# Moving stage d of the last three batches in the order of a fused transformer and RWKV block

## The chip, the core and the metric

The kernel runs on one core of a Trainium2 chip. The metric is the time of one execution on the device in microseconds, given as the median of several runs. One execution was also profiled; the lines quoted in this document come from its trace, in which time runs from the first instruction (0) to the last one (the span).

The engines are called as in the profile: PE (TensorE, matmuls), PEld (its weight loads), DVE (VectorE), ACT (ScalarE), POOL (GpSimd) and SPq (the queue of SyncE, from which this kernel issues its DMAs).

## The reference

Eight sequences (batches) of 256 tokens with 512 channels pass through two layers. The first is a transformer block with self-attention, cross-attention and an MLP. The second, in which the change lies, has a time mixing with a recurrence over the tokens in 32 heads of 16 channels, and a channel mixing:

```python
xk, xw, xv, xr, xg = ...                      # mixes of the normed input and its shift
w = jnp.exp(-jnp.exp(time_decay + jnp.tanh(xw @ td_w1) @ td_w2))
r, k, v, g = xr @ Wr.T, xk @ Wk.T, xv @ Wv.T, silu(xg @ Wg.T)
def step(s, rkvw):
    a = k_t[..., :, None] * v_t[..., None, :]
    out = jnp.einsum('bhi,bhij->bhj', r_t, u * a + s)
    s = a + w_t[..., :, None] * s
    return (s, out)
og = groupnorm(out) * gn_w + gn_b
x1 = x + og * g @ Wo.T
xc = _ln(x1, ln2_w, ln2_b)
xk2, xr2 = xc + sx2 * ffn_maa_k, xc + sx2 * ffn_maa_r
rr = jax.nn.sigmoid(xr2 @ Wfr.T)
kk = jnp.square(jax.nn.relu(xk2 @ Wfk.T))
return x1 + rr * (kk @ Wfv.T)
```

## The kernel before, in words

All large products are made of three matmuls each (`mm3`, L189 to L193): both factors are split into a high and a low part. The attention and MLP stages of all batches come first; the two mixings of the second layer follow and overlap with the end of the MLP.

**Time mixing** (class `TimeMix`) has five stages for a batch b. `a` norms the input and makes the small mixing factors. `b` and `e` project gate, key, value, decay and receptance and store them in DRAM. The recurrence is cut into chunks of 16 tokens: `c` (from L695) computes inside all chunks at once on POOL (products `X`, L720 to L762) and DVE (their sums, L722 to L769). It loads the values into two staging buffers (`vh`, L708 and L709) and ACT copies them into `vt` (L710), which takes a buffer of the tag `in`. `c` stores its results in DRAM (`back`, L771 to L777). `d` (from L780) is "the stage between chunks": it carries the state from chunk to chunk. It loads the chunk decays `dd` (`dn`, L784) and transposes them on PE (L787, tile `wtp`), forms the chunks' updates with 256 small matmuls (L814, tile `up`), transposes the receptance (`to_t`, L223 and L823, tile `wtp` again), scans over the chunks on DVE (L831), multiplies with 256 small matmuls (L841), adds to `c`'s output (L844), norms by heads (L850 to L868) and stores `yg` (L854).

**Channel mixing** (class `ChannelMix`) has six units for a batch: `p` (gate and transposes of `yg`), `o` (output projection, residual, norm), `t` (transposes and the two mixes, L937 to L943; the mix for `fr` is written to a tile `o`, the one for `fk` in place), `r` (product with `fr`, L950), `k` (product with `fk`, L959 to L962) and `v` (product with `fv`, L970 and L971). `p0` also loads the four weight matrices.

**What sets the order.** The program is written down stage by stage in the order of the string `SEQ` (L71). A compile-time scheduler then fixes each engine's order by priorities: a stage's priority is that of its batch plus its entry in `AT` (L86), so that `d` of batch b goes ahead of all channel mixing, and `p` to `v` follow by batch. Two things are added. `in_turn` (L874) puts the PE instructions of `o`, `t`, `r`, `k` and `v` behind the last matmul of the unit written before it, with `tc.issue_after`, which fixes the order of issue on PE and adds no wait for the end. And buffers are shared by tags: `SLOTS` (L54) and `BANKS` (L77) give each tile of a stage a tag, most with one buffer; `wst` is a pool of two buffers with one tag. The tags that matter here:

- PSUM bank k5: `wtp` of stage `d` (four tiles for a batch) and `o` of the unit `t` (two tiles).
- pool `wst` (`staged`, L543): two tiles `vh` of each `c`; five tiles of each `d`: `dn`, two tiles with the values (L799 to L801, loaded in L692), two with the receptance (L821).
- tag `in` (a16 to a19): three inputs and `vt` of each `c`, with one buffer each.

In the order before, `d5` stands between `c6` and `c7`, `d6` after `o0`, `d7` after `r0`, and no PE instruction of a `d` stands behind a unit.

Of the kernel before, what the change touches and what calls it, by code (L numbers as in the profile page):

```python
# [1 line left out]

# [15 lines left out]
P = 128  # L18
# [21 lines left out]
def slots(text):  # L40
# [28 lines left out]


SEQ = (  # L71
# [3 lines left out]
)  # L75

# [15 lines left out]
def r32(ap):  # L92
    return ap.bitcast(F32)
# [3 lines left out]
def block_kernel(ctx: ExitStack, tc: tile.TileContext, a: dict, out: bass.AP):  # L97
    nc = tc.nc
    NB = out.shape[0]
    V, S, G, TE = nc.vector, nc.scalar, nc.gpsimd, nc.tensor  # L100
# [12 lines left out]
    ident = r32(identr)  # L113
# [19 lines left out]
    def wt(name, shape, dt=F32):  # L133
        tag = name
        if name in SLOTS[phase[0]]:
            tags = SLOTS[phase[0]][name]
            i = turn.get((phase[0], name), 0)
            turn[phase[0], name] = i + 1
            tag = tags[i % len(tags)]
        return wk.tile(shape, dt, name=name, tag=tag)  # L140

    def bank(kind, shape):
        kind = {"attn": {"tp": "mm", "o": "mm", "out": "mm"}, "time": {"mp": "tp"}}.get(phase[0], {}).get(kind, kind)
        tags = BANKS[phase[0]][kind]
        i = turn.get((phase[0], kind, "bank"), 0)
        turn[phase[0], kind, "bank"] = i + 1
        return psp.tile(shape, F32, name=kind, tag=tags[i % len(tags)])
# [39 lines left out]
    latest = [None]  # L187
# [26 lines left out]
            V.tensor_scalar(xn[:, t, :], x[:, t, :], mv[:, t, 0:1], rstd[:, t : t + 1], ALU.subtract, ALU.mult)  # L214
        return xn

    def to_t(xn, emit, kind="tp"):

        for k2 in range(2):
            tp = bank(kind, [P, 2, T])  # L220
            for kk in range(2):
                for t in range(2):
                    latest[0] = TE.transpose(tp[:, kk, t * P : (t + 1) * P], xn[t][:, (2 * k2 + kk) * P : (2 * k2 + kk + 1) * P], ident)  # L223
            emit(k2, tp)

    def both(x):
# [196 lines left out]
    class SelfAttention:  # L423
# [23 lines left out]
        def d(self, b, cx):  # L447
            if b == 0:
                W[0, "row"] = load_row("bao")
            x = load_x(a["x"][b], "xr")  # L450
            add_row(x, W[0, "row"])
            residual_out([W[0, "o"]], [cx], x, x1[b])
# [75 lines left out]
            residual_out(self.w2, hs, x, x2p[b] if self.half == 0 else x3[b])  # L528


    def shifted(xc, st, b, sx):

        G.tensor_tensor(sx[:, :, 1:], xc[:, :, : T - 1], xc[:, :, 1:], ALU.subtract)
        G.tensor_tensor(sx[:, :, 0:1], st[:, :, b : b + 1], xc[:, :, 0:1], ALU.subtract)
        return sx
# [7 lines left out]
    def staged(shape):  # L543
        return wst.tile(shape, F32, name="w")

    class TimeMix:
# [233 lines left out]
        def d(self, b, got):  # L780

            ksd, r0d, dd, vd, ond = got
            dn = staged([16, D])
            nc.sync.dma_start(out=dn.rearrange("c (e d) -> c e d", e=8), in_=dd.rearrange("e c d -> c e d"))  # L784
            dt_ps = bank("wtp", [P, KC, 16])
            for k in range(KC):
                TE.transpose(dt_ps[:, k, :], dn[:, k * P : (k + 1) * P], ident[:16, :16])  # L787
            dts = wt("dts", [P, KC, 16])

            G.memset(dts[:, :, 0:1], 0.0)  # L790
            S.copy(dts[:, :, 1:16], dt_ps[:, :, 0:15])
            s0t = wt("s0t", [P, KC, 16])
            nc.sync.dma_start(out=s0t, in_=a["ctx"][b, 2:18, :].rearrange("r (a j) -> (r a) j", j=16).rearrange("(g p) j -> p g j", p=P))
            centred(s0t.rearrange("p g j -> p (g j)"), KC, bank("wtp", [P, KC]))
            ks = [self.n_tile(ksd, t, "ks") for t in range(2)]

            vms = []
            for t in range(2):
                vms.append(wt("vm", [P, 2, D]))  # L799
                vn = self.n_tile(vd, t)  # L800
                for par in range(2):  # L801
                    S.activation(vms[t][:, par, :], vn, AF.Copy, scale=pm[:, 2 + par : 3 + par])

            sts = wt("sts", [P, KC, 32, 16])
            for hp in range(2):
                S.activation(sts[:, :, 16 * hp : 16 * hp + 16, 0], s0t, AF.Copy, scale=pm[:, hp : hp + 1])
            for r_ in range(4):
                rws = slice(32 * r_, 32 * r_ + 32)
                up = bank("up", [P, 2, KC, 2, 32])
                for t in range(2):  # L810
                    for g in range(KC):
                        for q in range(4):
                            ch = slice(g * P + 32 * q, g * P + 32 * q + 32)
                            TE.matmul(up[32 * q : 32 * q + 32, t, g], ks[t][rws, ch], vms[t][rws, :, ch], start=True, stop=True)  # L814
                for t in range(2):
                    c0 = 1 + 8 * t + 2 * r_
                    n = min(2, 16 - c0)
                    for hp in range(2):
                        js = slice(16 * hp, 16 * hp + 16)
                        S.activation(sts[:, :, js, c0 : c0 + n].rearrange("p g j c -> p g c j"), up[:, t, :, 0:n, js], AF.Copy, scale=pm[:, hp : hp + 1])  # L820
            r0 = [self.n_tile(r0d, t) for t in range(2)]  # L821
            r0t = wt("r0t", [P, KC, T])
            to_t(r0, lambda k2, tp: S.copy(r0t[:, 2 * k2 : 2 * k2 + 2, :], tp), "wtp")  # L823
            o = wt("on_", [P, 2, D])
            for t in range(2):
                nc.sync.dma_start(out=o[:, t, :].rearrange("p (e d) -> p e d", e=8), in_=ond[:, t * P : (t + 1) * P, :].rearrange("e p d -> p e d"))
            for g in range(KC):
                dT = bank("up", [P, 32, 16])
                S.copy(dT, dts[:, g, :].unsqueeze(1).broadcast_to([P, 32, 16]))
                sv = sts[:, g].rearrange("p j c -> p (j c)")  # L830
                V.tensor_tensor_scan(sv, dT.rearrange("p j c -> p (j c)"), sv, 0.0, ALU.mult, ALU.add)  # L831

            for q in range(4):
                rws = slice(32 * q, 32 * q + 32)
                op = bank("up", [P, 2, KC, 32, 2])
                for t in range(2):
                    for g in range(KC):
                        for pr in range(4):
                            c0 = 8 * t + 2 * pr
                            at = t * P + 32 * pr  # L840
                            TE.matmul(op[32 * pr : 32 * pr + 32, t, g], r0t[rws, g, at : at + 32], sts[rws, g, :, c0 : c0 + 2], start=True, stop=True)  # L841
                ov = o.rearrange("p t (g q j) -> p (t g) q j", q=4, j=32)[:, :, q]
                for par in range(2):
                    V.scalar_tensor_tensor(ov, op.rearrange("p t g j c -> p (t g) j c")[:, :, :, par], pm[:, 2 + par : 3 + par], ov, ALU.mult, ALU.add)  # L844

            oh = heads(o)
            gn = bank("up", [P, 3, 64])
            for t in range(2):
                sq = wt("sq", [P, D])
                S.activation(sq, o[:, t, :], AF.Square)  # L850
                V.tensor_reduce(gn[:, 0, 32 * t : 32 * t + 32], sq.rearrange("p (h j) -> p h j", j=16), AX.X, ALU.add)
            r = rsqrt(gn)
            V.tensor_tensor(oh, oh, r.unsqueeze(2).broadcast_to([P, 64, 16]), ALU.mult)
            nc.sync.dma_start(out=tok(yg[b]), in_=o)  # L854
# [14 lines left out]
        return v  # L869


    last = [None]

    def in_turn(unit):  # L874

        with ExitStack() as turns:
            if last[0] is not None:
                turns.enter_context(tc.issue_after(last[0].ins))
            unit()
        last[0] = latest[0]  # L880

# [14 lines left out]
    class ChannelMix:  # L896
# [7 lines left out]

        def p(self, b):
            if b == 0:
                for n in ("o", "fr", "fk", "fv"):
                    W[n] = load_unit(a["w" + n])
                W["st0"] = wt("st0", [P, KC, NB])
                nc.sync.dma_start(out=W["st0"], in_=a["st0"])  # L910
            yn = wt("yn", [P, 2, D])
            nc.sync.dma_start(out=yn, in_=tok(yg[b]))
            g = wt("g", [P, KC, T])
            nc.sync.dma_start(out=g, in_=gt[b])
            self.yt[b] = yt = parts()

            def gated(k2, tp):
                ks = scaled(tp, k2, "gn")
                V.scalar_tensor_tensor(tp, tp, 0.5, g[:, ks, :], ALU.mult, ALU.mult)
                split_ps(yt, ks, tp)  # L920

            to_t(both(yn), gated)
# [138 lines left out]
```

## Time and profile before

| | |
|---|---|
| three runs | 1967.8, 1974.79, 1980.11 us |
| median | 1974.79 us |
| the profiled execution's own time | 1970.55 us |
| its span | 1968.8 us |
| mean granted clock of TensorE | 0.927 |
| busy: PE, DVE, ACT, POOL | 88%, 70%, 56%, 38% |

In the profile a line `L787 PE MATMUL wtp<-ident,w` names the line of the kernel, the engine, the operation, and the tile written and the tiles read (numbers at the end of names are left out, so `o` and `o2` read the same). `<-` behind an idle time names what ended it.

When the stages run: the starts of L787, one for each `d`, are at 1317, 1384, 1452, 1519, 1582, 1650, 1714 and 1755 us; the last reduction L769 of a `c` starts at 1578 (c4), 1648 (c5), 1711 (c6) and 1774.5 us (c7); `v` ends at 1781 for batch 0 and then about every 26 us, at 1965 for batch 7.

### The profile page before, as it was taken

Reading aid. Unit: us, or ns where it says so; the run is one execution under the profiler, and the core shown is the slowest. Engines: PE = TensorE matmul, PEld = TensorE weight load, DVE = VectorE, ACT = ScalarE, POOL = GpSimd, SP = SyncE. Lnnn points to the kernel's source line nnn. Section 1 sums busy time; section 2 is a strip of 40 time slices with the busy share of each in tenths; the row PEclk is TensorE's granted clock in tenths of the full one; section 3 lists DMA queues with packets and bytes.
Section 4 is the critical chain, followed back from the end, with each engine's and each line's share of the span. In section 5 each row is a group of like instructions: output and inputs, shape, how many; then the busy total and the mean of one; then the engine's idle time right before and its main releaser. Section 6 shows DMA issues by size and latency. Waiting matters only on the chain.

```text
span 1968.8 us, 38833 instructions
## 1 busy us (share of the span) xinstructions
PE 1722.7 (88%) x14576; PEld 1450.2 (74%) x14576; DVE 1376.8 (70%) x3211; ACT 1104.7 (56%) x2745; POOL 745.0 (38%) x550
## 2 busy tenths in 40 slices
PE   4999999999899998999999998888798885279997
PEld 4777777777787776799999986676677664267876
DVE  4777777776778687655654344669779887688664
ACT  3877777887778787632332334344454455254553
POOL 2111111121222221222321100798999999990000
PEclk9999999999999998999999998989898877578999
DMA  6744444656555557322311123364556577434331
GB/s 189 166 121 119 119 118 124 186 147 164 131 144 137 150 129 208 111 79 79 115 65 65 54 102 108 106 163 136 156 138 164 145 199 230 138 93 129 114 101 54
DMA packets 241521, 255.74 MB, mean 130 GB/s; under 512 B 156547, under 2 KB 159499, under 8 KB 241334
## 3 DMA queue, kind: packets, MB, share of 16 engines
q1 hardware_dynamic: 241334, 253.26, 46.4%
q8 instruction: 115, 1.88, 0.4%
q14 instruction: 72, 0.59, 0.1%
HBM read 122.91 MB, written 63.18 MB: 95 GB/s over the span
## 4 chain that ended last, share of the span: by engine, by line
PE 56%; DVE 15%; POOL 12%; DMA 5%; ACT 5%; issue 4%; SPq 3%; DVEq 0%; POOLq 0%; ACTq 0%
POOL X L762 7%; PE o L192 7%; PE o L191 7%; PE o L193 7%; PE mm L191 5%; PE mm L192 4%; PE mm L193 4%; PE tr L372 3%; PE out L193 3%; PE out L192 3%; PE out L191 3%; DVE e L365 3%; PE cx L381 2%; DVE e L363 2%; PE sc L361 2%
## 5 line engine op out<-in xcount | busy, mean ns | idle before, releaser
L368 ACT ACTIVATE e<-e,mx 128x256 f32<-128x256 f32 x512 | 256.8, 506 | 43.3 <-DVE mx L365 42.3
L363 DVE TENSOR_TENSOR e<-sc,mc 128x512 f32<-128x512 f32 x256 | 172.5, 685 | 106.8 <-PE sc L361 55.9
L233 POOL TENSOR_TENSOR u<-y,u 128x1024 fp32r<-128x1024 f32 x32 | 78.4, 2449 | 440.4 <-ACT u L232 410.3
L365 DVE CUSTOM_DVE_ANT_0 e<-e,mn 128x256 f32<-128x256 f32 x512 | 223.3, 480 | 1.0
L762 POOL TENSOR_TENSOR X<-A,in 128x128 f32<-128x128 f32 (+14 forms) x120 | 209.3, 1784 | 5.5 <-DVE ob L769 3.5
L372 PE MATMUL tr<-ident,e 128*128 128x128 f32 x1024 | 174.0, 285 | 17.3 <-ACT e L368 14.2
L191 PE MATMUL mm<-u,whi 128*128 128x256 f32 x512 | 154.3, 302 | 13.1 <-DVE s L325 6.6
L376 ACT COPY pt<-tr 128x512 f32<-128x512 f32 x256 | 146.7, 581 | 31.8 <-PE tr L372 31.0
L372 PEld LDWEIGHTS tr<-ident,e 128*128 128x128 f32 x1024 | 122.1, 144 | 48.0 <-ACT e L368 23.1
L191 PE MATMUL o<-whi,s 128*128 128x512 f32 x320 | 137.6, 430 | 15.8 <-ACT s L639 8.4
L192 PE MATMUL mm<-u,whi 128*128 128x256 f32 x512 | 147.4, 288 | 4.0 <-POOL u L233 4.0
L191 PE MATMUL o<-u,whi 128*128 128x256 f32 x512 | 144.5, 286 | 3.5 <-ACT whi L175 2.1
L193 PE MATMUL mm<-u,wlo 128*128 128x256 f32 x512 | 147.5, 288 | 0.0
L192 PE MATMUL o<-u,whi 128*128 128x256 f32 x512 | 144.0, 282 | 0.0
L193 PE MATMUL o<-u,wlo 128*128 128x256 f32 x512 | 143.9, 283 | 0.0
L299 POOL TENSOR_TENSOR xr<-xr,row 128x512 f32<-128x512 f32 x48 | 64.8, 1371 | 187.5 <-DMA xr<-in_x 81.0
L361 PE MATMUL sc<-stk 128*128 128x256 f32 x512 | 117.3, 321 | 21.1 <-DVE e L363 16.0
L192 PE MATMUL o<-wlo,s 128*128 128x512 f32 x320 | 133.4, 417 | 0.0
L193 PE MATMUL o<-whi,s 128*128 128x512 f32 x320 | 129.8, 416 | 0.8 <-DVE s L894 0.8
L514 ACT ACTIVATE hf<-o,cv 128x256 f32<-128x256 f32 x128 | 59.7, 474 | 118.0 <-PE o L193 115.2
L203 POOL TENSOR_SCALAR rstd<-mv 128x2 f32<-128x2 f32 x48 | 15.7, 327 | 275.7 <-DVE mv L201 256.8
L744 POOL TENSOR_TENSOR X<-in 128x1024 f32<-128x1024 f32 x48 | 113.0, 2375 | 9.8 <-DVE A L750 9.8
(324 smaller groups left out, 5220.7 us busy)
## 6 DMA issues: line engine op xcount, KB each, us to landing
stk<-s SPq DMA_DIRECT2D x512, 128.0 KB, 2.4
x<-x SPq DMA_DIRECT2D x56, 512.0 KB, 4.4
x<-xr SPq DMA_DIRECT2D x24, 512.0 KB, 3.5
xr<-x SPq DMA_DIRECT2D x16, 512.0 KB, 4.7
w<-in_w SPq DMA_DIRECT2D x16, 512.0 KB, 6.7
w<-v SPq DMA_DIRECT2D x32, 256.0 KB, 2.9
x<-in_x SPq DMA_DIRECT2D x8, 512.0 KB
xr<-in_x SPq DMA_DIRECT2D x8, 512.0 KB, 3.7
```

Source lines behind the costliest of these rows:

```text
L191: TE.matmul(o, ah, bh, start=first, stop=False)
L192: TE.matmul(o, ah, bl, start=False, stop=False)
L193: latest[0] = TE.matmul(o, al, bh, start=False, stop=last)
L233: (eng or V).tensor_tensor(lo, y, r32(hi), ALU.subtract)
L361: TE.matmul(sc[:, t, :], qs[hm][:, hc, t * P : (t + 1) * P], ks[hm][:, hc, :], start=True, stop=True)
L363: V.tensor_tensor(e, sc, mc, ALU.mult)
L365: V.tensor_tensor_reduce(e[:, t, :], e[:, t, :], mn[:, t, :], 1.0, 3.0e38, ALU.add, ALU.min, accum_out=mx[:, kk2, hc, t : t + 1])
L368: S.activation(pr[:, t, :], e[:, t, :], AF.Exp, bias=mx[:, kk2, hc, t : t + 1], scale=-1.0, accum_out=sums[:, kk2, hc, t : t + 1])
L372: TE.transpose(pt_ps[:, kk, t * P : (t + 1) * P], pr[:, t, kk * P : (kk + 1) * P], ident)
L376: S.copy(pt, pt_ps)
L744: G.tensor_tensor(X.rearrange("p (i s d) -> p i s d", i=ni, s=m), rb[:, t0 : t0 + ni, :].unsqueeze(2).broadcast_to([P, ni, m, 64]), kb[:, ...
L762: G.tensor_tensor(Y.rearrange("p (h j s) -> p h j s", h=4, j=16), A[:, t, 0:n, :].rearrange("p s h -> p h s").unsqueeze(2).broadcast_to([P ...
```

## The change

Four things change.

- `SEQ`: `d5` moves from between `c6` and `b7` to after `p1` (so after `c7`), `d6` from after `o0` to after `r1`, and `d7` from after `r0` to after `r3`.
- `behind()` is taken out of `in_turn` and made a function; it is empty as long as no unit has been written down.
- In `d`, every PE instruction (L787, L814, the transposes of `to_t` and L841) is now issued behind the last matmul of the unit written last before it: nothing for `d0` to `d4`, `o0` for `d5`, `r1` for `d6`, `r3` for `d7`.
- `p0` loads the weights in the order o, fk, fr, fv instead of o, fr, fk, fv.

```diff
-    "a0 b0 a1 e0 c0 b1 a2 e1 c1 d0 b2 a3 e2 c2 d1 b3 a4 e3 c3 d2 b4 a5 e4 c4 d3 b5 a6 e5 c5 d4 b6 a7 e6 c6 d5 b7 "
-    "e7 c7 p0 o0 d6 p1 t0 o1 p2 k0 r0 d7 t1 v0 o2 p3 k1 r1 t2 v1 o3 p4 k2 r2 t3 v2 o4 p5 k3 r3 "
+    "a0 b0 a1 e0 c0 b1 a2 e1 c1 d0 b2 a3 e2 c2 d1 b3 a4 e3 c3 d2 b4 a5 e4 c4 d3 b5 a6 e5 c5 d4 b6 a7 e6 c6 b7 "
+    "e7 c7 p0 o0 p1 d5 t0 o1 p2 k0 r0 t1 v0 o2 p3 k1 r1 d6 t2 v1 o3 p4 k2 r2 t3 v2 o4 p5 k3 r3 d7 "
     "t4 v3 o5 p6 k4 r4 t5 v4 o6 p7 k5 r5 t6 v5 o7 k6 r6 t7 v6 k7 r7 v7"
...
-    def to_t(xn, emit, kind="tp"):
+    def to_t(xn, emit, kind="tp", behind=nullcontext):
...
-                    latest[0] = TE.transpose(tp[:, kk, t * P : (t + 1) * P], xn[t][:, (2 * k2 + kk) * P : (2 * k2 + kk + 1) * P], ident)
+                    with behind():
+                        latest[0] = TE.transpose(tp[:, kk, t * P : (t + 1) * P], xn[t][:, (2 * k2 + kk) * P : (2 * k2 + kk + 1) * P], ident)
...
+    last = [None]
+
+    def behind():
+
+        return nullcontext() if last[0] is None else tc.issue_after(last[0].ins)
...
-                TE.transpose(dt_ps[:, k, :], dn[:, k * P : (k + 1) * P], ident[:16, :16])
+                with behind():
+                    TE.transpose(dt_ps[:, k, :], dn[:, k * P : (k + 1) * P], ident[:16, :16])
...
-                            TE.matmul(up[32 * q : 32 * q + 32, t, g], ks[t][rws, ch], vms[t][rws, :, ch], start=True, stop=True)
+                            with behind():
+                                TE.matmul(up[32 * q : 32 * q + 32, t, g], ks[t][rws, ch], vms[t][rws, :, ch], start=True, stop=True)
...
-            to_t(r0, lambda k2, tp: S.copy(r0t[:, 2 * k2 : 2 * k2 + 2, :], tp), "wtp")
+            to_t(r0, lambda k2, tp: S.copy(r0t[:, 2 * k2 : 2 * k2 + 2, :], tp), "wtp", behind)
...
-                            TE.matmul(op[32 * pr : 32 * pr + 32, t, g], r0t[rws, g, at : at + 32], sts[rws, g, :, c0 : c0 + 2], start=True, stop=True)
+                            with behind():
+                                TE.matmul(op[32 * pr : 32 * pr + 32, t, g], r0t[rws, g, at : at + 32], sts[rws, g, :, c0 : c0 + 2], start=True, stop=True)
...
     def in_turn(unit):
-        with ExitStack() as turns:
-            if last[0] is not None:
-                turns.enter_context(tc.issue_after(last[0].ins))
+        with behind():
             unit()
         last[0] = latest[0]
...
-                for n in ("o", "fr", "fk", "fv"):
+                for n in ("o", "fk", "fr", "fv"):
```

More of the change, by code (lines that the diff above doesn't have):

```diff
@@ L1 @@
-from contextlib import ExitStack
+from contextlib import ExitStack, nullcontext
 import concourse.bass as bass
@@ L869, in rsqrt @@
         return v
-    last = [None]
     def in_turn(unit):
-        with ExitStack() as turns:
-            if last[0] is not None:
-                turns.enter_context(tc.issue_after(last[0].ins))
+        with behind():
             unit()
```

## The prediction

> **What bounds the kernel now.** First the 40 slices of the page (49.2 us each), to find where TensorE (PE) is not full.
>
> ```profile
> PE   4999999999899998999999998888798885279997
> ...
> POOL 2111111121222221222321100798999999990000
> PEclk9999999999999998999999998989898877578999
> ```
>
> PE is full but for the slices from about 1600 to 1770 us. There POOL is full: it computes the chunks (stage c) of the last batches, and the chain that ended last runs through POOL's `X L762` until 1774.5 us and through PE from there on. So there are two regimes: POOL sets the pace until c7 ends, then the channel mixing's units on PE do. The busy times by stretch say how empty PE is in between:
>
> ```profile
> 1650.00:1700.00 50.00, 22.89 (x556) 18.52 (x556) 35.92 (x60) 19.95 (x48) 49.84 (x39) 0.60 0.58 171
> 1700.00:1750.00 50.00, 19.11 (x543) 16.45 (x544) 31.23 (x45) 16.89 (x38) 47.70 (x33) 0.53 0.25 71
> 1750.00:1800.00 50.00, 45.95 (x704) 39.91 (x704) 43.69 (x86) 28.80 (x64) 25.43 (x16) 0.86 0.54 156
> 1800.00:1850.00 50.00, 47.05 (x260) 40.06 (x259) 37.56 (x81) 26.23 (x53) 1.85 (x4) 1.00 0.36 115
> ```
>
> PE, PEld, DVE, ACT and POOL stand in this order, then the granted clock. Next, what PE waits for between 1600 and 1800 us (total, times, longest):
>
> ```profile
> PE wtp L787 <- DMA w<-dd: 37.6, 2, 26.1
> PE up L841 <- DVE sts L831: 12.6, 5, 5.1
> ```
>
> L787 is the first PE work of stage d. Taken alone the line says that d5 and d6 stand in front of a queue that could otherwise run. So I looked at what would run (the unit t0) and at why the load of `dd` is late: the timelines of DVE, ACT and the DMA queue.
>
> ```profile
> 1660.31 0.68 DVE L939 TENSOR_TENSOR xs<-tp,xs 128x510 f32<-128x510 f32 x1
> ...
> 1734.89 0.47 DVE L943 SCALAR_TENSOR_TENSOR o<-xs,cv,tp 128x256 f32<-128x256 f32 x1
> ```
>
> ```profile
> 1711.31 1.94 ACT L710 COPY in<-w 128x512 f32<-128x512 f32 x2 [17.46 <-POOL X L762]
> ...
> 1732.18 0.58 ACT L823 COPY r0t<-wtp 128x512 f32<-128x512 f32 x1
> ```
>
> ```profile
> 1648.71 0.33 SPq L784 DMA_DIRECT2D w<-dd  x1
> ...
> 1674.12 0.81 SPq L709 DMA_DIRECT2D w<-v  x2
> ...
> 1712.40 0.32 SPq L784 DMA_DIRECT2D w<-dd  x1
> ...
> 1713.27 0.37 SPq L692 DMA_DIRECT2D w<-v  x1
> ```
>
> Two things are to be seen. t0's L943 writes a tile of PSUM bank k5, the bank of d's `wtp`; t0 had all else at 1661 and ran at 1734.9, after d6 (traced before it) read its last `wtp` (L823, to 1732.8). k0, the next unit, starts at 1740.8. And `dd` of d6 was in DRAM from 1688.6, but its load (L784) went out at 1712.4, just after c7's L710 had read the two staging buffers of `wst`. So did d6's values (L692, 1713.3), stored by e6 long before, though d6 has the better priority than c7 and two buffers came free at 1674: c7's pair, traced earlier, took them. Buffers of a tag are given out in the order of the program's text, and L710 waits for c6's last POOL work, whose `in` buffer it takes over.
>
> **The change, part by part.** *d5 after c7 and p1.* Before, d5's five loads into `wst` stood between c6's pair and c7's; now c7's pair stands ahead of them. c7's pair can load at about 1649 (after c6's L710), but is read only when c6 ends, at 1711.3. So d5's L784 goes from 1648.7 to about 1712.4, with L692, L793 and L826 of d5 behind it, and d5 takes the place that d6 had: first PE work at 1714, last `wtp` read at 1732.8. d5 is still traced before t0, so t0 still waits for k5 until 1732.8 and k0 still starts at about 1740. PE between 1664 and 1713 loses d5's work and stays empty: the hole isn't filled. Gain until 1740: none; c6 took 63.5 us on POOL with d5 beside it and c7 63.2 with d6 (first L720 to the last L762), so I give POOL nothing.
>
> *d6 and d7 behind units.* d6's transposes and matmuls stand behind r1, d7's behind r3. With d6 and d7 gone from 1755 to 1804.5 us (the end of r1 before), PE saves d7's pieces between its unit matmuls, read from one start to the next: 0.35 (L787), 1.28, 1.25, 2.23, 1.03 (L814 and transposes), 3.24 and 1.91 (L841): 11.3 us. t1 no longer waits for d7's `wtp` (its L943 stood at 1775.8), which saves the stall in k1 and the slow matmuls behind it:
>
> ```profile
> 1785.16 0.58 PE L191 MATMUL o<-s,whi 128*128 128x256 f32 x1 [3.33 <-DVE x L926]
> ```
>
> 3.3 us, and 26 matmuls after it that came 0.213 us apart instead of 0.119: 2.4 us. Together 17.0 us, so r1 ends at 1787.5 instead of 1804.5. [...]
>
> From r1 to the end took 1968.8 - 1804.5 = 164.3 us before. That stretch now holds all of d6 and d7 as well. Work of one d on PE at full clock: 256 matmuls of L814 (128 in 1.89), 256 of L841 (128 in 2.1), transposes 8 x 0.1 and 4 x 0.07: 3.8 + 4.2 + 0.8 + 0.3 = 9.1 us. Beside it comes a stall s each: d's first PE instruction now waits in order behind r1, and t2's L943 waits for k5 until d6's last L823, so k2, and all that is queued behind it in the turn (r2, t3, v2, o4), waits too; likewise t4 and k4 for d7. d7's own rows before give the length: L787 at 1755.3, last L823 to 1773.2, second half of k1 at 1785.2: 29.9 us. In that time PE has dt 0.3, L814 3.8, transposes 0.8, t2 1.0, v1 5.8, o3 5.8 and six matmuls of k2 0.7: 18.2 us. Empty: 11.7, and 2.4 for the slow clock after it: s = 14.1 at most by these rows. From below: d's work can also fall into gaps that PE has anyway; in the 164 us from 1805 it was busy 147.3, so 16.7 are free, 8.3 for each d: s = -8.3. I take s = 7, nearer to d7's rows because it is the same chain: L841's 4.2 us may stand in the gap, and c7's reductions (L769, L750) no longer stand between t2's DVE steps, some 3 us: 11.7 - 4.2 - 3 + 2.4 = 6.9.
>
> Off PE, each d brings DVE and ACT work into a unit period: DVE had 19.5 of 26 us and ACT 13.6 there, and one d adds on DVE 4 scans x 1.22, 8 x 0.48 (L844), 2 x 0.68 (L851), 13 x 0.23 and 1.22: 14.3. 33.8 in 26 + 9.1 + 7 us is covered. c7 itself now has room: d7 can't start before r3. r3 ended at 1856.7 before, so 1856.7 - 17.0 + 16.1 = 1855.8.
>
> *fk ahead of fr.* Same four DMAs of 512 KB in another order; the last weight was split by 1656 (L176), k0 starts at 1740. Nothing; only if nothing else held k0 back would it count, by the time between the two pairs (L175 copied fr's last half until 1630, fk's until 1641).
>
> **Sum.** Span 1968.8 - 17.0 + 2 x (9.1 + 7) = 1984.0, +15.2. The profiled execution took 1970.55 and the median of the three runs is 1974.79; adding 15.2 to the median: 1990.
>
> [...]
>
> **Rivals.**
> 1. *d5 keeps its time* (faster). If c7's pair does not hold the staging buffers, d5 runs at 1650 and frees k5 at 1677.4 (its last L823) instead of 1732.8. Everything from t0 on comes 55.4 us earlier: 1990 - 55 = 1935. For it: only that the two buffers were empty at 1648.5. Against it: d6's loads in the same situation. It decides if L784 of d5 goes out before c6 ends.
> 2. *d6 and d7 cost their full chain* (slower): s = 14.1, span 1998.2, so 2004.
> 3. *d6 and d7 vanish in PE's gaps*: s = -8.3, span 1953.4, so 1959. Against it: 3.4 us of the gaps are in one place, before the last k.
> 4. *d7 ends too late for o7*: o7 started 58.7 us after r3, so 1855.8 + 58.7 + 16.1 = 1930.6. From L787 to the store of `yg` a d took 51 to 67 us (d4, in a busy PE, 67), then 4.5 to load, about 7 in p7: 1918 to 1934. Over 63 us it counts; 3.7 us at 67: 1994.
>
> **How the numbers follow.** Likeliest 0.45 (own range 1978 to 2002, set by s from 1 to 13), rival 1 0.13, rival 2 0.26, rival 3 0.10, rival 4 0.06. Under 1% this kernel's measurement can hardly tell from no change: 1955 to 1994.5 is "same". Rival 1 is faster, and 0.01 of rival 3; the likeliest lies two thirds under 1994.5 (0.30) with rival 3's 0.09 and 0.01 of rival 4: 0.40. Slower: 0.15 + 0.26 + 0.05 = 0.46. The range leaves out rival 1 and little above rival 2, and takes in rival 3: 1959 to 2010.
>
> **What would show it.** Right: d5's L787 near 1714, L943 of t0 near 1735, PE empty from 1665 to 1713, r1 ending near 1788, d6's L814 after it and a stall before k2, d7's L841 near 1885. Wrong: L787 of d5 near 1650 or L943 before 1700 (rival 1); PE without gaps around k2 and k4 (rival 3); PE waiting before o7 (rival 4).

## The result, and the profile after

| | before | after |
|---|---|---|
| median of seven runs each, same chip | 1974.79 us | 1987.51 us |
| lowest to highest | 1967.8 to 1984.6 | 1983.93 to 1995.11 |
| the profiled execution's own time | 1970.55 us | 1994.46 us |
| its span | 1968.8 us | 1992.7 us |

The ratio after to before is 1.0067, 95% interval 1.0038 to 1.0097: slower by 12.7 us in the medians, against a forecast of 15.2. In the kernel after, the lines of stage `d` and of the mixes are 6 to 10 higher: L795 is the first PE work of a `d` (before: L787), L791 the load of `dd` (L784), L716 and L717 c's pair of loads and its copy (L709, L710), L823 the small sums `up` (L814), L832 the copy of the receptance (L823), L851 the last products (L841), L949 t's mixes (L943), L776 c's reductions (L769).

One caution ahead of the numbers. The two profiled executions differ by 23.9 us, of which the medians show 12.7: that of before lay 4 us under its median, that of after 7 over. The last reduction of c5 ends at 1649.1 us before and at 1654.5 after, and what lies ahead of it is not what the change is about. So I also compare the stretch from there to the end of the span, called *the tail* here: 319.7 us before, 338.2 after, +18.5. Where an absolute time is needed I take off 5.2 us (c6's end on POOL: 1711.3 and 1716.5).

First the slices of the page, after:

```profile
PE   4999999999999998999999988888788881289997
...
POOL 2111111122211221332211101999999999970000
PEclk8999999999999998999999999998889875589999
```

The hole in PE is still there under a full POOL, and deeper: its two emptiest slices have 1 and 2 tenths, where before had 5 and 2. The same stretches of busy time as in the prediction (PE, PEld, DVE, ACT, POOL, then the clock):

```profile
1650.00:1700.00 50.00, 8.62 (x32) 6.60 (x32) 26.24 (x37) 10.80 (x19) 49.84 (x37) 0.57 0.44 145
1700.00:1750.00 50.00, 16.89 (x476) 14.50 (x476) 27.00 (x36) 18.49 (x40) 48.41 (x30) 0.52 0.26 64
1750.00:1800.00 50.00, 42.75 (x265) 36.33 (x265) 41.38 (x82) 20.51 (x39) 29.95 (x21) 0.86 0.40 138
1800.00:1850.00 50.00, 46.38 (x705) 39.70 (x705) 36.52 (x77) 28.88 (x66) 1.03 (x3) 0.93 0.44 119
```

From 1650 to 1700 PE has 8.6 us of work instead of 22.9: d5 has left. From 1800 to 1850 it has 705 instructions instead of 260: d6 has come. What PE waits for from 1640 to 1900 us:

```profile
PE wtp L795 <- DMA w<-dd: 52.4, 1, 52.4
PE tp L224 <- ACT yn L211: 15.4, 2, 14.5
PE up L851 <- DVE sts L840: 9.9, 4, 7.6
```

Two waits for `dd` (37.6 us) have become one of 52.4: d5's. The timelines of the DMA queue, of ACT, of DVE and of PE tell it step by step.

```profile
1654.11 0.33 SPq L716 DMA_DIRECT2D w<-v  x1
...
1655.01 0.42 SPq L716 DMA_DIRECT2D w<-v  x1
```

```profile
1717.61 0.32 SPq L791 DMA_DIRECT2D w<-dd  x1
1718.48 0.38 SPq L699 DMA_DIRECT2D w<-v  x1
```

```profile
1716.51 1.94 ACT L717 COPY in<-w 128x512 f32<-128x512 f32 x2 [37.89 <-POOL X L769]
...
1733.92 0.61 ACT L832 COPY r0t<-wtp 128x512 f32<-128x512 f32 x1
```

```profile
1736.74 0.47 DVE L949 SCALAR_TENSOR_TENSOR o<-xs,cv,tp 128x256 f32<-128x256 f32 x1
```

```profile
1719.40 0.61 PE L795 MATMUL wtp<-ident,w 16*128 16x16 f32 x4 [52.40 <-DMA w<-dd]
...
1745.83 0.56 PE L191 MATMUL o<-s,whi 128*128 128x256 f32 x1
...
1799.95 0.42 PE L795 MATMUL wtp<-ident,w 16*128 16x16 f32 x4
...
1867.07 0.42 PE L795 MATMUL wtp<-ident,w 16*128 16x16 f32 x4
...
1885.15 1.92 PE L851 MATMUL up<-sts,r0t 32*32 32x64 f32 x128
```

c7's pair takes both staging buffers at 1654 and sits on them until ACT reads it at 1716.5, when c6 ends; 1.1 us later d5's load goes out. t0's mix follows d5's last `wtp`, k0 follows at 1745.8, and d6 and d7 stand right behind r1 (1799.95) and r3 (1867.07).

### The profile page after: what moved, and what is told of

The parts are those of the page before. It is cut to its first block, busy times and chain, and to the rows that moved or that the text cites. A ratio compares the mean times of both kernels' runs of the same rounds, so it can differ in the third digit from the quotient of the medians.

```text
span 1992.7 us, 38832 instructions
## 1 busy us (share of the span) xinstructions
PE 1724.2 (87%) x14576; PEld 1451.9 (73%) x14576; DVE 1377.6 (69%) x3211; ACT 1104.9 (55%) x2745; POOL 744.7 (37%) x550
## 4 chain that ended last, share of the span: by engine, by line
PE 55%; DVE 17%; POOL 8%; ACT 6%; DMA 6%; issue 4%; SPq 3%; DVEq 0%; ACTq 0%; POOLq 0%
PE o L191 6%; PE o L192 6%; PE o L193 6%; POOL X L769 5%; PE mm L191 5%; PE mm L192 5%; PE mm L193 4%; PE tr L373 3%; PE out L193 3%; PE out L192 3%; PE out L191 3%; DVE e L366 3%; PE cx L382 2%; DVE e L364 2%; PE sc L362 2%
## 5 line engine op out<-in xcount | busy, mean ns | idle before, releaser
L769 POOL TENSOR_TENSOR X<-A,in 128x128 f32<-128x128 f32 (+14 forms) x120 | 208.6, 1784 | 7.0 <-DVE ob L776 5.0
L373 PE MATMUL tr<-ident,e 128*128 128x128 f32 x1024 | 172.9, 283 | 16.7 <-ACT e L369 13.7
L203 POOL TENSOR_SCALAR rstd<-mv 128x2 f32<-128x2 f32 x48 | 16.7, 347 | 268.7 <-DVE mv L201 249.8
L191 PEld LDWEIGHTS mm<-u,whi 128*128 128x128 f32 x512 | 100.3, 196 | 22.4 <-DVE s L326 11.5
```

Of the source, the lines that this page charges most:

```text
L191: TE.matmul(o, ah, bh, start=first, stop=False)
L373: TE.transpose(pt_ps[:, kk, t * P : (t + 1) * P], pr[:, t, kk * P : (kk + 1) * P], ident)
L769: G.tensor_tensor(Y.rearrange("p (h j s) -> p h j s", h=4, j=16), A[:, t, 0:n, :].rearrange("p s h -> p h s").unsqueeze(2).broadcast_to([P ...
```

## The experiments

Each kernel was profiled and timed in rounds against the kernel before on the same chip; the ratios below are to the kernel before. The end of c5's last reduction and the tail of each profile (from there to the end) stand beside the median. c5's end moved by up to 16 us from kernel to kernel, and the end of c4 ahead of it by nearly as much (1571.9 to 1586.5), though up to c4's end the engines and the DMA queue run the same instructions in the same order in all of them. So where two kernels are compared by absolute times below, this drift has to be taken off; each tail is that of one execution.

| kernel | median us | ratio, 95% interval | c5's end us | tail us |
|---|---|---|---|---|
| before | 1974.8 | | 1649.1 | 319.7 |
| after | 1987.5 | 1.0067 [1.0038, 1.0097] | 1654.5 | 338.2 |
| 1 d5 back | 1950.3 | 0.9872 [0.9838, 0.9906] | 1648.7 | 294.1 |
| 2 own staging | 1941.0 | 0.9824 [0.9789, 0.9858] | 1648.4 | 288.5 |
| 3 d free of the units | 1973.5 | 0.9982 [0.9961, 1.0002] | 1643.2 | 321.5 |
| 4 before, fk first | 1974.1 | 0.9985 [0.9967, 1.0004] | 1647.6 | 321.1 |
| 5 = 1 and 3 | 1944.0 | 0.9838 [0.9809, 0.9866] | 1653.0 | 288.0 |
| 6 = 2 and 3 | 1947.9 | 0.9855 [0.9832, 0.9879] | 1658.9 | 288.3 |
| 7 mix in bank k6 | 2012.5 | 1.0181 [1.0154, 1.0208] | 1656.3 | 355.6 |
| 8 only `up` free | 1990.1 | 1.0075 [1.0049, 1.0101] | 1656.1 | 334.6 |
| 9 mix in bank k0 | 1960.9 | 0.9927 [0.9899, 0.9955] | 1649.8 | 305.7 |
| 10 only transposes free | 1995.6 | 1.0104 [1.0078, 1.0130] | 1651.3 | 341.6 |
| 11 = 2 and 9 | 1962.4 | 0.9934 [0.9911, 0.9957] | 1654.8 | 305.8 |
| 12 before, own staging | 1968.9 | 0.9976 [0.9956, 0.9995] | 1653.9 | 319.1 |

**1. d5 put back.** The changed kernel with d5 between c6 and b7 again; d6 and d7 as changed.

```diff
-  ... e6 c6 b7 e7 c7 p0 o0 p1 d5 t0 o1 ...
+  ... e6 c6 d5 b7 e7 c7 p0 o0 p1 t0 o1 ...
```

> The kernel after with d5 written where it stood before (between c6 and b7, ahead of c7); d6, d7, behind() and the order of the weights stay as after. My theory (c7's pair of loads holds the two staging buffers, so d5 waits for c6's end, and t0 waits for d5's wtp in bank k5): d5's first PE work at about 1650 instead of 1719 us, k0 some 55 us earlier, r1 about 1745, r3 about 1812, end about 1937 in the trace, median about 1935. The rival (PE's order alone decides, d5's place in the text does not matter): within 5 us of after, about 1987.

Measured: 1950.31 us, 37 us under after. d5's L795 stands at 1650.0, t0's first mix at 1678.0, and r1 ends at 1740 instead of 1800.

```profile
1650.03 0.61 PE L795 MATMUL wtp<-ident,w 16*128 16x16 f32 x4 [12.96 <-DMA w<-dd]
```

From there to r3 it takes 74.9 us instead of 67.1. The mechanism held, the size of the gain fell short of 52 us.

**2. A staging buffer of its own for c7's pair.** The changed order is kept; only the last batch's `vh` no longer comes from `wst`.

```diff
-                vh = staged([P, 8, 64])
+                vh = wk.tile([P, 8, 64], F32, name="vh", tag="b9") if b == NB - 1 else staged([P, 8, 64])
```

> The kernel after, but c7 loads its values through another buffer (tag b9), one after the other, instead of the two staging buffers; all orders in the text stay as after. My theory: with the staging buffers free, d5 starts at about 1650 though it is written after c7, so the time is near that of the run with d5 back, about 1935. The rival (it is d5's place in the text as such, by bank k5 or by PE's order, and not the staging buffers): about 1987.

Measured: 1940.99 us, the fastest kernel of this study. d5 now starts where it did before the change, though it is written after c7 and p1. Its rows of the DMA queue, of PE and of DVE:

```profile
1646.62 0.42 SPq L791 DMA_DIRECT2D w<-dd  x1
```

```profile
1650.61 0.60 PE L795 MATMUL wtp<-ident,w 16*128 16x16 f32 x4 [11.21 <-DMA w<-dd]
```

```profile
1676.54 0.48 DVE L949 SCALAR_TENSOR_TENSOR o<-xs,cv,tp 128x256 f32<-128x256 f32 x1
```

And the stretches of the same kernel:

```profile
1650.00:1700.00 50.00, 35.91 (x625) 30.91 (x626) 39.89 (x65) 27.98 (x63) 48.02 (x37) 0.66 0.62 181
1700.00:1750.00 50.00, 42.95 (x445) 35.90 (x444) 39.08 (x72) 27.75 (x63) 47.94 (x30) 0.90 0.40 122
1750.00:1800.00 50.00, 43.15 (x437) 36.40 (x435) 49.02 (x100) 21.24 (x42) 28.62 (x22) 0.86 0.52 163
```

PE fills 78.9 of the 100 us from 1650 to 1750, where after had 25.5. From 1750 to 1800 DVE is full instead (49.0 of 50): c7's reductions, until 1787, stand beside the channel mixing. The edit has a price too: c7 ends 138.7 us after c5 instead of 128.1. Its two halves now go through one buffer one after the other, and d5 and the units run beside it; the run doesn't tell the two apart.

**3. Nothing of d held behind a unit.** The changed text order, but `behind()` empty in `d`; `in_turn` keeps its order for the units.

```diff
     def behind():
-        return nullcontext() if last[0] is None else tc.issue_after(last[0].ins)
+        return nullcontext()
...
-        with behind():
+        with nullcontext() if last[0] is None else tc.issue_after(last[0].ins):
             unit()
```

> The kernel after without behind() around stage d's PE instructions; the units keep their turn. My theory: d6 and d7 come on PE as soon as the bank k5 is free of the t units written before them, a few us to 20 us earlier than behind r1 and r3, so 1975 to 1990, at most 10 us under after. The rival (the issue order behind r1 and r3 is what costs the 13 us): back to 1975 or below.

Measured: 1973.5 us, 14 us under after (the tail 16.7 under), which is the rival's outcome and not mine. The whole loss of the change is gone, with d5 still late. On PE, d6 now stands ahead of r1's end (1790.0):

```profile
1774.85 0.42 PE L795 MATMUL wtp<-ident,w 16*128 16x16 f32 x4 [0.86 <-DVE s L900]
```

```profile
1786.57 0.48 PE L851 MATMUL up<-sts,r0t 32*32 32x64 f32 x32
```

r1 to r3 takes 60.2 us (after 67.1, before 52.2), r3 to the end 114.5 (after 125.6, before 112.1). From 100 to 150 us after c5's end PE was busy for 47.9 of the 50 us, in after for 44.2: work of d6 fits into PE's gaps there. c5's end to r1 grew by 1.3 us only (146.8, after 145.5).

**4. Only fk ahead of fr**, in the kernel before.

```diff
-                for n in ("o", "fr", "fk", "fv"):
+                for n in ("o", "fk", "fr", "fv"):
```

> The kernel before with the one edit that fk's weights are loaded ahead of fr's. My theory: nothing, since k0 starts 90 us after the last load: 1975, within 5 us. Rival: the loads' order on the DMA queue delays or speeds something else by more than 10 us.

Measured: 1974.14 us. Nothing that can be told from no change.

**5 and 6. Do the two gains add?** Experiments 1 and 2, each with the edit of 3 on top.

```diff
     def behind():
-        return nullcontext() if last[0] is None else tc.issue_after(last[0].ins)
+        return nullcontext()
```

> The changed kernel with d5 put back between c6 and b7, and with nothing of d's held behind a unit. Theory (two causes, which add: d5's staging buffer, and the issue of d6's and d7's matmuls behind r1 and r3): the 14.0 us that the second alone gave off the changed kernel come off the 1950.3 of d5 put back too: about 1936 (1930 to 1942). Rival (freed from the unit, d6's matmuls only gained where c7's staging delayed the start; with d5 early they have no slack): about 1950.

> The changed kernel with c7's pair of loads staged in a buffer of its own, and with nothing of d's held behind a unit. Theory (the two causes add): 1941.0 less 14.0, about 1927 (1921 to 1933). Rival (they do not add): about 1941.

Measured: 1944.04 us with d5 back, 6 under experiment 1; 1947.87 with the own staging, 7 over experiment 2. In both pairs the intervals of the ratios overlap, and the tails say -6.1 and -0.2, where experiment 3 had -16.7. The gains do not add, and my theory that they do fell. d6's L795 did come forward, by 10 and 14 us counted from c5's end, as it did in experiment 3 (14), and r3 to the end shrank by 11 and 10 us (11 in experiment 3). But c5's end to r3, which in experiment 3 became 5.6 us shorter, became some 5 and 10 longer here: what d7 saves behind r3 it costs ahead of it. PE's idle time in that stretch says the same: experiment 3 took it from 82.4 us (after) to 73.9, while here it went from 37.0 to 36.0 and from 30.4 to 31.7. So freed work of d filled gaps only where many were left. Why the 30 to 37 us of idle time that remain take up none of it, no run shows. DVE is not full there in these two kernels: from 100 to 150 us after c5's end it was busy for 40.7 and 41.5 of the 50 us.

**7. Another bank for t's second mix: k6.** The changed kernel, with one entry of `BANKS` changed.

```diff
-    "chan": slots("tp:k2,k4 o:k5 o2:k1,k3,k0"),
+    "chan": slots("tp:k2,k4 o:k6 o2:k1,k3,k0"),
```

> The changed kernel with t's second mix in bank k6 instead of k5. Theory (c7's staging loads hold d5's four transposes, which stand ahead of k0 on TensorE): t0's mix may go some 50 us earlier, but k0 still waits behind d5's transposes and sums, which start near 1719; k0 begins at 1735 to 1742 instead of 1746, the time is 1978 to 1988. Rival (bank k5 alone holds t0 and with it k0): k0 near 1690, about 1935.

Measured: 2012.49 us, 25 us worse than after, and expected by neither theory. k6 is one of the two banks of `up`, in which d also puts its last products; so t0's mix no longer waits for d5's transposes but for its last products to be read (L854, to 1753.7). The rows of PE and DVE of this kernel:

```profile
1721.17 0.60 PE L795 MATMUL wtp<-ident,w 16*128 16x16 f32 x4 [52.43 <-DMA w<-dd]
```

```profile
1753.78 0.49 DVE L949 SCALAR_TENSOR_TENSOR o<-xs,cv,tp 128x256 f32<-128x256 f32 x1
```

L949 goes 32.6 us after d5's L795, 17.3 in after. It repeats behind d6 (L795 at 1804, t2's mix near 1836 instead of 1811). The bank does hold the mix; I had chosen one that is held for longer.

**8. Only the small sums free of the unit.** The changed kernel, `behind()` off L823 alone.

```diff
-                            with behind():
+                            with nullcontext():
                                 TE.matmul(up[32 * q : 32 * q + 32, t, g], ...
```

> The changed kernel with only the 128 small sums of each d (the block up) free of the unit; its four transposes, the transposes of r0 and the last products stay behind r1 and r3. Theory 1 (what costs is the TensorE time of these sums between the units): the two blocks of sums go into gaps, 4 to 7 us less for each: about 1977. Theory 2 (what costs is bank k5, which the next mix gets only after r0's transposes): still about 1987.

Measured: 1990.13 us, as after (the tail 3.6 under it). d6's sums went to 1761 to 1784, into gaps, and next to nothing came of it.

**9. t's second mix in bank k0**, which no part of d uses. The matrix sums lose their third bank.

```diff
-    "chan": slots("tp:k2,k4 o:k5 o2:k1,k3,k0"),
+    "chan": slots("tp:k2,k4 o:k0 o2:k1,k3"),
```

> The changed kernel with t's second mix in bank k0, which no part of d uses, instead of k5; the matrix sums of the channel mixing share two banks in place of three. c7's pair of loads still stages as in the changed kernel, so d5's transposes still start near 1719. Theory (bank k5 is what holds t0's mix and k0 behind d5): t0's mix and k0 start near 1690 as with d5 put back, d5's sums fall into later gaps, about 1945 (1930 to 1960). Rival (c7's work on VectorE and GpSimd sets the end, whatever t0 does): 1975 to 1990. A third (two banks in place of three cost at each unit): over 1990.

Measured: 1960.85 us, ratio 0.9927 [0.9899, 0.9955], 27 us under after. d5's transposes are as late as in after (1720.9), and t0's mix no longer waits for them. The rows of PE and of DVE:

```profile
1664.84 1.15 PE L191 MATMUL o<-s,whi 128*128 128x256 f32 x2 [2.30 <-ACT s L899]
...
1720.86 0.42 PE L795 MATMUL wtp<-ident,w 16*128 16x16 f32 x4 [2.96 <-DMA w<-dd]
```

```profile
1658.66 0.49 DVE L949 SCALAR_TENSOR_TENSOR o<-xs,cv,tp 128x256 f32<-128x256 f32 x1
```

k0 begins at 1664.8, 81 us ahead of after's (76 counted from c5's end), now ahead of d5's transposes on PE, and r1 ends at 1727. Part of it is given back twice: d5's sums and last products now lie behind r1, and r1 to r3 takes 94 us (after 67.1); and behind r3, where the stores of the last five results come 27.3 us apart instead of 25.4 in experiment 2, r3 to the end takes 134.9 us instead of 125.3. I put the second down to the two banks in place of three; no run parts it from the mix's own place in k0.

**10. Only the transposes free of the unit** (L795 and those of L832), the rest held.

```diff
-                with behind():
+                with nullcontext():
                     TE.transpose(dt_ps[:, k, :], dn[:, k * P : (k + 1) * P], ident[:16, :16])
...
-            to_t(r0, lambda k2, tp: S.copy(r0t[:, 2 * k2 : 2 * k2 + 2, :], tp), "wtp", behind)
+            to_t(r0, lambda k2, tp: S.copy(r0t[:, 2 * k2 : 2 * k2 + 2, :], tp), "wtp")
```

> The changed kernel with d's four transposes and the transposes of r0 (those that use bank k5) free of the unit; the small sums up and the last products stay behind r1 and r3. Theory 2 of the run before (bank k5 reaches the next mix only after r0's transposes): most of the 14 to 16 us that freeing everything gave, about 1975. Rival (it is the last products, or all of it together): about 1987.

Measured: 1995.58 us, 8 us over after (the tail 3.4 over). No gain, so the theory that bank k5 behind r1 makes the 14 us fell too: here t2's mix ended at 1810 instead of 1821, and the store of v2 stood at 1849, as in after. What experiments 8 and 10 share with after, and not with experiment 3, is where d6's last products start. PE in after, in 8 and in 10:

```profile
1814.16 0.54 PE L851 MATMUL up<-sts,r0t 32*32 32x64 f32 x24 [0.31 <-DVE sts L840]
```

```profile
1814.88 0.49 PE L851 MATMUL up<-sts,r0t 32*32 32x64 f32 x32
```

```profile
1813.82 0.54 PE L851 MATMUL up<-sts,r0t 32*32 32x64 f32 x24 [1.00 <-DVE sts L840]
```

1814 in all three; 1786.6 in experiment 3. Counted from c5's end that is 159.7, 158.8 and 162.5 us, and 143.4 in experiment 3. They need the sums, both sets of transposes and the scans, so one of these left behind r1 keeps them behind it. That is what the rows show; a kernel with the last products alone freed was not tried, so which of d's parts must go ahead for the 14 us stays open.

**11. Own staging and bank k0 together.**

```diff
-                vh = staged([P, 8, 64])
+                vh = wk.tile([P, 8, 64], F32, name="vh", tag="b9") if b == NB - 1 else staged([P, 8, 64])
...
-    "chan": slots("tp:k2,k4 o:k5 o2:k1,k3,k0"),
+    "chan": slots("tp:k2,k4 o:k0 o2:k1,k3"),
```

> c7's pair of loads staged in a buffer of its own, and t's second mix in bank k0 instead of k5. Theory (d's stages hold the next mix through bank k5 also after c7's staging no longer holds d5): a few us under the 1941.0 of the own staging alone, about 1932 (1925 to 1941). Rival (PE has no more waits there to win, and two banks in place of three cost): 1941 to 1955.

Measured: 1962.43 us, 21 us worse than the own staging alone and over both ranges. Counted from c5's end k0 starts 11 us earlier than with the own staging alone (21.8 instead of 33.3), but r1 ends where it did (90.9, 90.7): with d5 early the bank has nothing left to give. Behind that the edit costs, as in experiment 9: r1 to r3 takes 80.4 us instead of 72.5, r3 to the end 134.5 instead of 125.3.

**12. The order of before with c7's own staging**: the edit of 2 alone, in the kernel before.

```diff
-                vh = staged([P, 8, 64])
+                vh = wk.tile([P, 8, 64], F32, name="vh", tag="b9") if b == NB - 1 else staged([P, 8, 64])
```

> The kernel before, with its own order, and only c7's pair of loads staged in a buffer of its own. Theory (the loads that stand in the queue of staging buffers hold d6's transposes, and with them k0): d6's transposes go near 1690 instead of 1714, k0 starts near 1715 instead of 1741: about 1950 (1940 to 1962). Rival (it is the place of d6 and d7 ahead of k0 and k1 that holds k0, not the staging): 1970 to 1976.

Measured: 1968.93 us, ratio barely under 1; the tail is 0.6 us under that of before. That is nearer to the rival than to my 1950. d6's transposes moved from 1714 to 1703.8 and t0's mix from 1734.9 to 1721.4, the way the theory says though less far, but the gain didn't last. The DVE rows of t0's and of t1's mix:

```profile
1721.44 0.46 DVE L943 SCALAR_TENSOR_TENSOR o<-xs,cv,tp 128x256 f32<-128x256 f32 x1
```

```profile
1781.72 0.46 DVE L943 SCALAR_TENSOR_TENSOR o<-xs,cv,tp 128x256 f32<-128x256 f32 x1
```

t1's mix stands at 1781.7 (before: 1776), still behind d7, which is written ahead of it and whose transposes went at 1762 (before: 1755). r1 ends 152.7 us after c5's end, 2.7 earlier than before, and the rest gives 2 of them back. So the four kernels with and without each edit are:

| | order of before | order of after |
|---|---|---|
| staging shared | 1974.8 | 1987.5 (ratio 1.0067) |
| c7's pair staged apart | 1968.9 (0.9976) | 1941.0 (0.9824) |

Each alone is worth -6 or +13 us, both together -34 (by the tails -0.6, +18.5 and -31.2). The new order takes d6 and d7 out of the way of t0 and t1, but pushes d5 behind c7's staging; only without that does the first count.

## Why the prediction was right

**No gain until k0: right, and shown.** d5's L795 was to go near 1714, and went at 1719.4 (1714.2 less the 5.2); t0's mix near 1735, and went at 1736.7 (1731.5); k0 "at about 1740", and began at 1745.8 (1740.6). Experiments 1 and 2 show that c7's staging is the cause of d5's late start, and experiments 7 and 9 that bank k5 is what hands the delay on to t0. The head of PE's queue is not enough by itself: in 9, with d5 as late, k0 ran 76 us earlier counted from c5's end, ahead of d5 on PE.

**r1's end 17.0 us earlier: too much.** It ended at 1800.0, or 1794.8 less the 5.2, and not at 1787.5: 9.7 us earlier. With d7 gone its pieces on PE went, 11.3 us by my sum. The stall of k1 and the slow matmuls behind it (3.3 and 2.4) did not. I had put them on d7's transposes alone; now t1's mixes stood among c7's reductions on DVE, which last until 1782.6:

```profile
1772.25 0.48 DVE L949 SCALAR_TENSOR_TENSOR o<-xs,cv,tp 128x256 f32<-128x256 f32 x1
1772.64 1.01 DVE L776 TENSOR_REDUCE ob<-X 128x64 f32<-128x832 f32 x1
1774.76 0.48 DVE L949 SCALAR_TENSOR_TENSOR o<-xs,cv,tp 128x256 f32<-128x256 f32 x1
1775.15 1.08 DVE L776 TENSOR_REDUCE ob<-X 128x64 f32<-128x896 f32 x1
...
1781.36 1.21 DVE L776 TENSOR_REDUCE ob<-X 128x64 f32<-128x1024 f32 x1
```

On PE, two matmuls of k1, a gap, and from 1785.15 on matmuls 0.213 us apart instead of 0.119, at a granted clock of 0.50:

```profile
1781.73 0.50 PE L191 MATMUL o<-s,whi 128*128 128x256 f32 x2 [1.80 <-ACT s L899]
1784.33 0.63 PE L224 MATMUL tp<-ident,yn 128*128 128x128 f32 x4 [2.10 <-issue]
```

17.0 less 5.7 is 11.3; 9.7 was measured. Two readings of mine were off as well, by too little to matter: the row before has 20 steps of 0.213 us and not 26, so the slow matmuls were some 1.9 us and not 2.4, and 1688.6 is when the store of d6's `dd` was issued, not when it was done.

**d6 and d7 cost 9.1 us of PE and a stall of 7 each: right in kind and nearly in size, wrong in what the 7 is made of.** r1 to the end grew from 164.3 to 192.7 us, by 28.4 and not by 32.2: r1 to r3 by 14.9, r3 to the end by 13.5. Less 9.1 each that is 5.8 and 4.4 beside d's work, inside the bounds of -8.3 and 14.1. The stretches r1 to r3 and r3 to the end, before and then after, with two short ones of after (columns as above, the clock behind POOL):

```profile
1804.50:1856.70 52.20, 49.25 (x275) 42.06 (x274) 37.16 (x77) 27.24 (x54) 1.85 (x4) 1.00 0.41 132
1856.70:1968.80 112.10, 98.52 (x528) 83.43 (x526) 64.35 (x126) 47.11 (x92) 2.78 (x6) 0.98 0.23 75
```

```profile
1800.00:1867.10 67.10, 61.95 (x798) 52.99 (x797) 47.77 (x98) 38.52 (x85) 1.96 (x5) 0.95 0.48 136
1867.10:1992.70 125.60, 111.90 (x1053) 94.92 (x1052) 77.70 (x156) 56.36 (x119) 2.78 (x6) 0.93 0.22 74
1826.10:1832.90 6.80, 6.10 (x29) 6.10 (x30) 4.73 (x11) 4.70 (x11) 0.93 (x2) 0.50 0.82 257
1873.90:1880.70 6.80, 6.80 (x124) 5.86 (x114) 3.47 (x6) 4.92 (x14) 0.00 (x0) 0.50 0.02 5
```

PE's idle time grew by 2.2 and 0.1 us, its busy time by 12.7 and 13.4. d's own matmuls and transposes fill 9.4 and 10.0 us of that, read from one start to the next; the rest is the units' work, which took 3.3 and 3.4 us longer, with a stretch at a granted clock of 0.50 behind each of r1 and r3. My 7 had 4.5 us of an empty PE and 2.4 of the slow clock in it; it is rather the other way round. Nor do PE's waits stand in front of k2 and k4, where I had put them on bank k5: those that came new are mainly 2.7 us in front of d6's last products (L851) and 1.6 us for d7's receptance. Experiment 3 shows that most of the 28.4 us comes with the issue behind r1 and r3, not with the place in the text: without it the two stretches take 18.0 us less, and r1 to r3 runs at a clock of 1.00. That part of d's work needs no time of its own is my rival 3 (hidden in PE's gaps); the gaps that took it lie ahead of r1 and r3, where the change forbids d to use them.

**The sum.** -9.7 + 28.4 = 18.7 between the profiles with the 5.2 off, 12.7 between the medians, 15.2 forecast. The two errors, 7.3 too much gain and 3.8 too much loss, partly cancel; that the number came out within 3 us is in part luck.

**fk ahead of fr: nothing**, as experiment 4 shows.

**The rivals.** Rival 1 did not happen, but experiments 1 and 2 make it happen: r1 then ends at 1740, 55 us earlier than after's 1794.8 without its drift, as priced. The medians gain only 37 and 47 us (the tails 44 and 50): my price let a delay at the front go through to the end whole, but r1 to r3 then takes 74.9 and 72.5 us instead of 67.1. c7's reductions fall into that stretch now; that they are the reason was not shown. Rival 2 (the full chain) and rival 4 (d7 late for o7) did not come: yg of d7 was stored at 1908, and from 1900 on PE has no wait for it.

**The wait at the head.** Taken alone, the 37.6 us at the head of PE's queue looked like a gain of as much. In after no matmul ran on PE from 1667 to 1719.4, while L795 waited. Yet the change lost 12.7 us: the wait at the head was the mark of a buffer that was late, and with d5 in d6's place it grew to 52.4 us.

## What to carry to other kernels

Before moving a stage, list the buffers and banks that it shares with its new neighbours, and ask for each who is now ahead of it in the order of the text and how long that one holds it: here two staging buffers, held for 62 us by a load that was early for nothing, decided more than the move. A change that loses can be one half of a change that wins: the new order was worth +13 us, the staging edit -6 (by the tail -0.6), both -34, so test the edits in pairs. And a fixed order of issue costs what the scheduler, left free, would have put into the gaps ahead of it (14 us here), but only while there are such gaps: with the staging mended, freeing d gave 6 us at most in one kernel and nothing in the other.

## What the runs showed of the hardware

The stretch ahead of the change moved between kernels whose instructions stand in the same order there: c4's last reduction ended at 1578.0 us in experiment 2 and at 1586.5 in experiment 6, c5's at 1648.4 and 1658.9. Whether that belongs to the kernel or to the single execution, no run parts: the four timed runs of 6 agree within 1.6 us, the seven of the kernel before lie 16.8 us apart. A difference of 7 us between two profiles here need not come from the edit; the stretch around it says more than the total.

In after, PE went on at 1784.33 after the 2.1 us gap in k1, and its matmuls of 128x256 came at first 0.12 us apart (1784.91, 1785.03, 1785.15). From 1785.15 they came 0.213 us apart, until 1791.90, and 0.119 us apart from 1792 on: 6.7 us at the slow pace, with no wait over 0.3 us in between. The granted clock was 0.50 from 1785.1 to 1791.9 and 1.00 from 1792 to 1800. The slow stretch cost about 2 us (some 20 steps, each 0.094 longer); what set its length, no run shows.
